# Softmax maxima for one quad of channels in eight, kept on the chip instead of sent through memory for two; reordered start and end of a two-layer product-quantised convolution

## The chip, the cores and the metric

One core of one Trainium2 chip. The metric is device time in microseconds (us) of one execution; medians are over several executions on the chip. The kernel before takes 2812.78 us, the median of four runs (2811.74 in three of them). Verdicts are drawn at 2%, which is 56 us here.

The engines are called by their names: TensorE (PE in the profile), VectorE (DVE), ScalarE (ACT), GpSimd (POOL) and SyncE (SP). PSUM is the accumulator memory that TensorE writes, SBUF the on-chip memory that holds this kernel's other tiles. The granted clock is the share of TensorE's full clock that the profile records; at half clock it is 0.5.

## The reference

16 images of 256 channels and 28 x 28 positions. A convolution layer is replaced by a soft choice among 16 centroids per channel; two layers follow each other.

```python
def amm_conv3x3(x, centroids, w_sub):          # (B,256,28,28), (256,16,9), (256,9,256)
    p = patches3x3(x)                            # B, n=784, c=256, s=9
    d = sum(p*p) - 2 * einsum('bncs,cks->bnck', p, centroids) + sum(centroids**2)
    attn = softmax(-d, axis=-1)                  # over the 16 centroids
    lut  = einsum('cks,cso->cko', centroids, w_sub)
    return einsum('bnck,cko->bno', attn, lut)
xn = group_norm(x)                               # 32 groups of channels
out = relu(bn1(amm_conv3x3(xn, centroids1, wsub1)))
out = bn2(amm_conv3x3(out, centroids2, wsub2))
out = se_gate(out)                               # mean -> 16 -> 256 -> sigmoid, a scale per channel
return x + relu(out + xn)
```

The `sum(p*p)` term is the same for all centroids and drops out of the softmax. What has to be computed per position and channel is 16 logits, their exponentials, 9 weighted sums (called numerators) and one total.

## The kernel before

Each image and layer is cut into two position tiles (384 and 400 columns) and each of these into eight quads of channels. One quad of one tile is a *unit*, and the kernel advances one unit per *slot* of about 4.9 us. For a unit, TensorE computes the logits as a group of 32 small matmuls (32 x 32 tiles of the array) into two pairs of PSUM banks, ScalarE exponentiates, TensorE computes the numerators as another group of 32, VectorE transposes them out of PSUM, inverts the totals, GpSimd multiplies (`k`), VectorE transposes back (`q`), and TensorE multiplies `q` with the output weights into the accumulator ("looks", groups of 128 x 128 matmuls). Several units are in flight at once.

There are only three PSUM pairs, and logits and numerators take two each in turn:

```python
ring = [p_ring.tile([P, 2, 512], F32, name=f"pair{i}") for i in range(3)]
def pair():
    turn[0] += 1
    return ring[turn[0] % 3]
```

So the second half of a unit's logits always needs the pair that the first of the two numerator transposes (`nt<-pair` in the profile) of the unit ahead has emptied.

In the second layer the logits can be large, and for two quads of eight the exponentials need their maxima subtracted. The kernel before computes the logits of these units twice: once early to find the maxima, which go through memory and come back as two more rows of the patches (21 and not 19), and once more for use. Units whose maxima are subtracted are called *treated* below.

```python
if m in maxed:                                   # MAXED = (0, 4)
    a = s - self.lb                              # lb = 6 slots ahead
    at(a, MAX, a_logits, u);  at(a, MAX, a_turn, u)            # logits, transposed
    at(a + 1, TURN_BACK, a_max, u, 0)
    at(a + 2, TURN_BACK, a_max, u, 1);  at(a + 2, TURN_BACK, m_turn, u)
    at(a + 3, MOVE, m_out, u);  at(a + 4, MOVE, m_in, u)       # through memory
at(s, LOGITS, b_logits, u);  at(s, EXP, b_exp, u)              # again, with maxima
at(s + 1, NUM, b_num, u)
at(s + 1, TURN, b_turn, u);  at(s + 1, TURN, c_scale, u)       # nt, rc, k
at(s + 2, TURN_BACK, c_turn, u)                                # q
```

Within a slot the positions run in the order LOGITS, EXP, LOOK_A, NUM, TURN, LOOK_B, MAX, LOOK_C, TURN_BACK, REST.

## Time and profile before

| | before |
|---|---|
| median (with the changed kernel's runs) | 2812.78 us (2810.43 to 2818.25) |
| span of the profiled run, granted clock | 2814.8 us, 0.990 |
| busy: TensorE, VectorE, GpSimd, ScalarE | 98%, 80%, 63%, 39% |
| second-layer logits computed twice | 16 images x 2 tiles x 2 quads = 64 units |

```profile
PE acc L717 <- ACT im L729: 2.3, 1, 2.3
PE pair L585 <- DVE nt L665: 1.9, 3, 1.0
```

The first line holds the 64 extra groups (2048 of the 18432 matmuls). The wait of logits for the numerator transposes is 1.9 us in the whole run.

### The profile page before, as it was taken

What the parts mean: (1) busy time and instruction counts of PE and PEld (TensorE: products, weight loads), DVE (VectorE), ACT (ScalarE), POOL (GpSimd) and SP (SyncE); (2) the same over time, 40 slices, a digit from 0 to 9 for tenths busy, and PEclk for the clock granted to TensorE, in tenths of its full rate; (3) what the DMA queues carried; (4) which work ended last, traced back from release to release, by engine and by line L of the source; (5) the groups of instructions that cost most, each with busy time, mean ns of one, the idle gap of its engine ahead of it and who ended that gap; (6) DMA issues with size and microseconds to landing.
All of it is one profiled execution on the core that took longest, in us unless ns stands there. A gap on an engine that the chain in (4) does not pass through costs nothing.

```text
span 2814.8 us, 94692 instructions
## 1 busy us (share of the span) xinstructions
PE 2756.0 (98%) x39794; PEld 1090.2 (39%) x39794; DVE 2252.0 (80%) x2772; ACT 1086.5 (39%) x1595; POOL 1782.1 (63%) x2589
## 2 busy tenths in 40 slices
PE   6999999999999999999999999999999999999996
PEld 3333333333333343333333333343333334333332
DVE  4668788887878878788887878878788887878885
ACT  2333433434334343433434334343433434334332
POOL 3785666756666575665756667575665756665653
PEclk9999999999999999999999999999999999999998
DMA  8787878768687676777777687676777767674641
GB/s 223 205 202 193 234 204 225 194 169 219 155 226 195 167 212 165 214 184 191 191 175 218 159 222 195 169 214 161 215 189 191 190 170 221 161 210 106 163 122 55
DMA packets 292787, 525.83 MB, mean 187 GB/s; under 512 B 94096, under 2 KB 247552, under 8 KB 292352
## 3 DMA queue, kind: packets, MB, share of 16 engines
q0 software_dynamic: 51808, 269.48, 36.0%
q1 hardware_dynamic: 240544, 250.20, 34.5%
q8 instruction: 315, 5.16, 0.8%
q14 instruction: 120, 0.98, 0.1%
HBM read 267.87 MB, written 251.69 MB: 185 GB/s over the span
## 4 chain that ended last, share of the span: by engine, by line
PE 92%; DVE 3%; POOL 2%; DMA 2%; issue 1%; ACT 0%; SPq 0%; DVEq 0%; POOLq 0%; ACTq 0%
PE acc L717 58%; PE pair L585 17%; PE pair L653 15%; DVE nt L665 1%; POOL k L681 1%; DMA pt<-pat 1%; DVE q L699 0%; DMA pat<-side 0%; DVE rc L671 0%; PE pair L319 0%; DMA out_dram<-y 0%; POOL pat L486 0%; PE pair L514 0%; POOL total L693 0%; DVE gn_st L434 0%
## 5 line engine op out<-in xcount | busy, mean ns | idle before, releaser
L717 PE MATMUL acc<-q,ws 128*128 128x384 f32 (+1 forms) x4096 | 1645.9, 520 | 5.1 <-ACT y L739 2.8
L681 POOL TENSOR_TENSOR k<-nt,rc 128x832 f32<-128x832 f32 (+1 forms) x512 | 802.9, 1568 | 980.6 <-DVE rc L671 970.7
L665 DVE STREAM_TRANSPOSE nt<-pair 128x832 f32<-128x832 f32 (+1 forms) x1024 | 979.3, 994 | 487.3 <-PE pair L653 436.0
L643 ACT ACTIVATE e<-pair 128x800 f32<-128x800 f32 (+1 forms) x1024 | 787.5, 821 | 1356.8 <-PE pair L585 1303.2
L717 PEld LDWEIGHTS acc<-q,ws 128*128 128x128 f32 x4096 | 698.1, 190 | 903.2 <-issue 577.6
L585 PE MATMUL pair<-pt,wd 19*32 19x384 f32 (+2 forms) x18432 | 556.6, 501 | 11.4 <-DMA pt<-pat 8.2
L699 DVE STREAM_TRANSPOSE q<-k 128x832 f32<-128x832 f32 (+1 forms) x512 | 488.9, 955 | 0.8 <-POOL k L681 0.8
L653 PE MATMUL pair<-e,cw 32*32 32x384 f32 (+1 forms) x16384 | 485.5, 501 | 0.3 <-DVE nt L665 0.2
L671 DVE RECIPROCAL rc<-nt 128x104 f32<-128x104 f32 (+1 forms) x512 | 398.5, 778 | 17.6
L585 PEld LDWEIGHTS pair<-pt,wd 19*32 19x32 f32 (+1 forms) x18432 | 138.2, 103 | 339.8 <-issue 276.2
L687 POOL TENSOR_TENSOR tail<-nt,rc 128x104 f32<-128x104 f32 (+1 forms) x512 | 236.7, 462 | 0.0
L653 PEld LDWEIGHTS pair<-e,cw 32*32 32x32 f32 x16384 | 119.9, 103 | 289.5 <-issue 154.8
L717 PE MATMUL acc<-qt,ws 128*128 128x400 f32 (+1 forms) x512 | 219.3, 510 | 0.0
L693 POOL TENSOR_TENSOR total<-total,nt 128x96 f32<-128x96 f32 (+1 forms) x448 | 197.4, 441 | 0.0
L486 POOL DMA_DIRECT2D pat<-side x274 | 184.7, 674 | 3.5 <-ACT side L475 3.0
L693 POOL TENSOR_TENSOR total<-total,rc 128x96 f32<-128x96 f32 (+1 forms) x448 | 176.1, 393 | 0.0
L717 PEld LDWEIGHTS acc<-qt,ws 128*128 128x128 f32 x512 | 91.1, 190 | 100.1 <-issue 50.3
L609 DVE TENSOR_REDUCE mx<-z 128x48 f32<-128x768 f32 (+1 forms) x128 | 120.6, 942 | 0.0
L604 DVE STREAM_TRANSPOSE z<-pair 128x768 f32<-128x768 f32 (+1 forms) x128 | 118.1, 961 | 0.0
L486 POOL DMA_DIRECT2D pat<-im x136 | 92.0, 677 | 0.7 <-ACT side L475 0.6
L739 ACT ACTIVATE y<-acc,bnsh,bnsc 128x384 f32<-128x384 f32 (+1 forms) x64 | 43.3, 677 | 87.3 <-PE acc L717 81.6
L551 POOL TENSOR_TENSOR y<-y,xt 128x392 f32<-128x392 f32 x60 | 65.9, 1099 | 10.4 <-ACT y L547 10.4
(113 smaller groups left out, 720.5 us busy)
## 6 DMA issues: line engine op xcount, KB each, us to landing
pat<-side POOLq DMA_DIRECT2D x232, 588.0 KB, 6.0
pt<-pat SPq DMA_DIRECT2D x1024, 112.5 KB
pt<-pat SPq DMA_DIRECT2D x1024, 108.0 KB
pat<-im POOLq DMA_DIRECT2D x116, 588.0 KB, 5.9
xt<-in_x POOLq DMA_DIRECT2D x32, 784.0 KB, 8.1
out_dram<-y POOLq DMA_DIRECT2D x16, 784.0 KB, 6.1
pat<-side POOLq DMA_DIRECT2D x24, 300.0 KB, 5.3
pat<-side POOLq DMA_DIRECT2D x18, 288.0 KB, 5.5
```

The costliest lines, as they stand in the source:

```text
L486: eng.dma_start(view(pat, (ROWS * p0 + 9 * k + 3 * dx) * HW + px, [[ROWS * HW, m], [HW, 3], [1, n]]), bass.AP(v.tensor, v.offset, [list(v. ...
L585: nc.tensor.matmul(ps[t // 2][c : c + 32, t % 2, :n], lhsT=wd[l][32 * i : 32 * i + rows, 4 * u["m"] + t, :], rhs=u["pt"][32 * i : 32 * i + ...
L609: nc.vector.tensor_reduce(u["mx"][:, 2 * v : 2 * v + 2].rearrange("p t (j b) -> p t b j", j=2)[:, :, :nb], u["z"].pop(0)[:, : 64 * nb].rea ...
L643: nc.scalar.activation(e[:, :, :n], ps[:, :, :n], AF.Exp, scale=2.0)
L653: nc.tensor.matmul(u["nm"][t // 2][32 * i : 32 * i + 32, t % 2, :n], lhsT=cw[l][c : c + 32, 4 * u["m"] + t, :], rhs=es[t // 2][c : c + 32, ...
L665: nc.vector.transpose(nt[:, :nb, 2 * v : 2 * v + 2].rearrange("p b t r -> p t b r"), ps[:, :, : 32 * nb].rearrange("p t (b r) -> p t b r", ...
L671: nc.vector.reciprocal(rc[:, : 8 * nb], u["nt"][:, :, SUM])
L681: nc.gpsimd.tensor_tensor(q[:, :nb].rearrange("p b (a s) -> p (b a) s", s=8), nt[:, :, :8], rc.unsqueeze(2).to_broadcast([P, 8 * nb, 8]), ...
L687: nc.gpsimd.tensor_tensor(tails[key][:, :nb, 8 * (m % 4) : 8 * (m % 4) + 8], nt[:, :, 8].rearrange("p (b a) -> p b a", a=8), rc.rearrange( ...
L693: nc.gpsimd.tensor_add(t[:, : 8 * nb], t[:, : 8 * nb], v)
L699: nc.vector.transpose(q[:, :, : 32 * nb].rearrange("p h (b r) -> p h b r", r=32), u.pop("k")[:, :nb].rearrange("p b (h r) -> p h b r", h=2),)
L717: nc.tensor.matmul(accs[key][:, :n], lhsT=ws[l][:, 2 * m + h if h < 2 else 2 * NQ + m // 4, o * P : (o + 1) * P], rhs=u["q"][h][:, :n], st ...
```

## The change

The intent: treat one quad of eight and not two; compute its logits once, and subtract the maxima from the transposed copy on the chip; and trim the start (first image's normalisation ahead of the sorting of channels, first patches alone on the queues) and the end (last image gated and stored by block, the check of the sums moved ahead). A bar on the centroids lessens the logits so that the other quads stay in range without maxima.

```diff
-MAXED = (0, 4)
+MAXED = (0,)
...
                     if m in maxed:
                         a = s - self.lb
-                        at(a, MAX, a_logits, u)
+                        at(a, MAX, logits, u)
                         at(a, MAX, a_turn, u)
-                        at(a + 1, TURN_BACK, a_max, u, 0)
-                        at(a + 2, TURN_BACK, a_max, u, 1)
-                        at(a + 2, TURN_BACK, m_turn, u)
-                        at(a + 3, MOVE, m_out, u)
-                        at(a + 4, MOVE, m_in, u)
+                        for v in range(2):
+                            at(a + 1 + v, TURN_BACK, a_max, u, v)
+                            at(a + 2 + v, REST, a_less, u, v)      # GpSimd: z - max
+                        at(s - 1, TURN_BACK, a_back, u, 0)         # VectorE: transpose back
+                        at(s, EXP, a_back, u, 1)
+                        at(s, EXP, a_exp, u)                       # from SBUF
                     else:
                         self.loads.append((s - self.lead, s, u))
-                    at(s, LOGITS, b_logits, u)
-                    at(s, EXP, b_exp, u)
+                        at(s, LOGITS, logits, u)
+                        at(s, EXP, b_exp, u)
...
-    load_x(0, x[0])                                   # GpSimd's queue
+    load_x(0, x[0], nc.sync)
...                                                    # statistics ahead of the sorting
-    plan = Plan(1, 3, 6)
+    plan = Plan(1, 3, 5)
...
-            plan.prep(0, pat_of(0, b), {1: 9, ...}, 0.67 if b == 1 else 1)
+            if b == 1: plan.prep_near(0, pat_of(0, b), 9)      # second image's patches by tile
...
-    plan.at(14, REST, square_codes, 1)                # second codes' setup between slots
-    plan.at(15, REST, setup_codes, 1)
...                                                    # last image: close_last, store_block
```

Cut: the new sort key and bar, the placement of the second codes, the spreading of early patch writes, the guard's second program.

## The prediction

> **What bounds the kernel now.** I read the page first (busy shares), then TensorE's timeline in the middle of the run, then its waits, then VectorE's timeline beside it, and last the head and the tail.
>
> ```profile
> PE 2756.0 (98%) x39794; PEld 1090.2 (39%) x39794; DVE 2252.0 (80%) x2772; ACT 1086.5 (39%) x1595; POOL 1782.1 (63%) x2589
> ...
> PE 92%; DVE 3%; POOL 2%; DMA 2%; issue 1%; ACT 0%; SPq 0%; DVEq 0%; POOLq 0%; ACTq 0%
> ```
>
> TensorE carries 92% of the chain that ended last. A high busy share alone could hide gaps, so the timeline has to show whether groups follow each other without a hole. This is TensorE (start, duration) around one extra logits group of the second layer:
>
> ```profile
> 1599.01 1.61 PE L717 MATMUL acc<-q,ws 128*128 128x400 f32 x4
> 1600.55 0.95 PE L585 MATMUL pair<-pt,wd 19*32 19x400 f32 x32
> 1601.43 1.61 PE L717 MATMUL acc<-q,ws 128*128 128x400 f32 x4
> 1602.97 0.93 PE L585 MATMUL pair<-pt,wd 19*32 19x384 f32 x32
> ```
>
> No idle bracket. A logits group (32 instructions, 16 at a time) takes 0.88 us from start to next start at 400 columns, 0.86 at 384. An accumulation group of four takes 1.54 us; elsewhere six take 2.21, so two more cost 0.67 and each group pays about 0.21 us of entry beside its matmuls. The image period comes from the chain of work, where the same piece recurs every 169.21 us:
>
> ```profile
> 978.09 2.21 PE acc L717 x6
> ...
> 1147.30 2.21 PE acc L717 x6
> ...
> 1665.90 2.21 PE acc L717 x6
> 1835.11 2.21 PE acc L717 x6
> ```
>
> 16 x 169.21 = 2707 of the 2815 us. The other 107 us are head, tail and a few stalls. Per image: 68 groups of 32 at about 0.87 = 59; 144 looks at 0.655 = 94; 68 entries at 0.21 = 14; small norm and gate matmuls 1.4; sum 168.7. So the steady part has no stall to remove: a saving must be TensorE work.
>
> VectorE is second, with 80%. Its unit of work per slot (one tile of one quad, about 4.9 us of TensorE) is two transposes out of PSUM, a reciprocal, one transpose back:
>
> ```profile
> 1599.20 1.85 DVE L665 STREAM_TRANSPOSE nt<-pair 128x768 f32<-128x768 f32 x2 [0.77 <-PE pair L653]
> 1601.08 0.76 DVE L671 RECIPROCAL rc<-nt 128x96 f32<-128x96 f32 x1
> 1601.75 1.91 DVE L604 STREAM_TRANSPOSE z<-pair 128x832 f32<-128x832 f32 x2
> 1603.59 0.94 DVE L699 STREAM_TRANSPOSE q<-k 128x768 f32<-128x768 f32 x1
> ```
>
> It waits 0.77 us for TensorE before the pair: one and a bit us of slack in a quiet slot, no more. And where VectorE is late, TensorE does stop. This is the last image, where four gate operations came first:
>
> ```profile
> 2733.93 2.67 DVE L543 SCALAR_TENSOR_TENSOR y<-xt,gn_rstd,y 128x392 f32<-128x392 f32 x4
> 2736.53 1.83 DVE L665 STREAM_TRANSPOSE nt<-pair 128x768 f32<-128x768 f32 x2
> ...
> 2742.55 1.97 DVE L665 STREAM_TRANSPOSE nt<-pair 128x832 f32<-128x832 f32 x2
> ```
>
> ```profile
> 2742.25 0.90 PE L585 MATMUL pair<-pt,wd 19*32 19x400 f32 x16
> 2743.64 0.91 PE L585 MATMUL pair<-pt,wd 19*32 19x400 f32 x16 [0.49 <-DVE nt L665]
> 2744.48 1.56 PE L717 MATMUL acc<-q,ws 128*128 128x384 f32 x4
> ```
>
> The second half of the logits needs the PSUM pair that the first of the two transposes empties. The transposes began 0.30 us after the logits, so logits to next group took 2744.48 - 2742.25 = 2.23 us in place of 0.88: 1.35 us lost. This price list returns below.
>
> **What the Trainium skill says.** "TensorEngine Tiling (Array Packing)", Key Properties: changing the tiling mode drains the engine. The 0.21 us per group agrees, since every group here alternates between 32x32 and 128x128. The same page, PSUM Bottleneck: tiling speeds up TensorE but not the emptying of PSUM; the 2742 us lines show it. "TensorE: Matmul & The Clock Gate", What's actually happening: after an idle window of some 3.4 us the array runs at half clock until it has been busy about as long. The stretch 36 to 46 us has a granted clock of 0.5 to 0.6 after a 6 us wait for patches. "DMA: Bandwidth & Descriptors", Queues, rings and completion order: an engine takes packets from its queues in turn, so what shares the time with the first patches delays them; the trace (12.26 us from the last issue to landing) fits.
>
> **The change part by part.**
>
> *Second-layer maxima, TensorE.* Before, quads 0 and 4 each compute logits twice per tile: 16 images x 2 tiles x 2 quads = 64 extra groups. After, quad 0 alone is treated, and its only logits group is turned, lessened by its maxima, turned back and exponentiated from SBUF; quad 4 is plain. All 64 extra groups go, and with each one entry, since two look groups merge. 64 x (0.87 + 0.21) = 69 us off the path.
>
> *The same, VectorE.* Gone: 64 units x (1.85 transposes + 1.89 maxima + 0.31 small turn) = 259 us. Added or kept: 32 units x (1.85 + 1.85 + two transposes back, about 1.8) = 176. Net 83 us less, on average a relief. But it is not spread. The order of VectorE's instructions in the built new kernel puts both transposes back directly after one slot's regular work and directly ahead of the next slot's pair, while the next slot is also shorter, because it has no logits group. I work one such place out by hand. Let N be the start of the numerator group ahead of it, 400 columns. VectorE: pair at N+1.08 (as 1598.15 to 1599.20 above), reciprocal +2.01, transpose +0.72, then free +0.92: N+4.73. Two transposes back, 0.84 each at the spacing of the existing SBUF ones: N+6.41, and only then the next pair. TensorE: 0.88 + four merged looks 2.88 + numerator 0.88 + two looks 1.54: next logits at N+6.19. The transposes thus begin 0.2 to 0.3 us after the logits, the very case of 2742 us: first transpose 1.09, second half group 0.83, so the next group starts at N+8.33 in place of N+7.05. Loss 1.28 us; at 384 columns the same sum gives 1.27. 32 x 1.27 = 41 us back.
>
> *GpSimd.* Added: 64 subtractions of 128x832 at about 1.57 (as the k product, same shape) = 100 us, and 32 x 0.84 of totals for quad 4; 1782 becomes about 1900, 69% of the span. In the slots that also hold the residual and the store it lags about 1.2 us, and the second subtraction still ends about 1.2 us before it is needed. Off the path.
>
> *Transfers.* The 64 round trips of the maxima through memory go. They were hidden.
>
> *Head.* x leads SyncE's queue and the statistics come first on VectorE: apply at about 15.4 us in place of 18.25. Patches then share the engines with the other six patch writes instead of the next x: land at about 30 to 31 in place of 35.4. They still trickle into TensorE, some 4 us. Gain 4. Slots 0 to 5 keep their GpSimd wait for the centroid scratch (6.07 us) and the half clock: 1. The setup of the second codes (6 matmuls 1.88 us, wait 1.09) leaves TensorE at 137 to 140 us, but the patch loads that queue behind the centroid placements are already late there (wait 1.71 us, then half clock), and two placements are added: of 3.5 I credit 2.
>
> *Tail.* From the last gate at 2796.5 VectorE now has six operations at about 0.62 instead of eight (5.0 us): 1.3; the check of the sums moves ahead; the store goes by block from SyncE instead of after GpSimd's residual (2802.78) with 0.73 of issue: together about 4. Other waits around the first image: 1.5.
>
> Sum: -69 + 41 - 4 - 1 - 2 - 4 - 1.5 = -40.5 us from 2811.7, so about 2770, or 1.5% less.
>
> **The rivals.**
>
> First, no new stall: VectorE's load falls, and the author spread the work over five slots. Then -69 and the ends give about 2730 (2.9% less). For it: 80% busy, waits of 0.8 to 2.4 us in quiet slots. Against it: the order of instructions and the 1.35 us already seen. Half the stall gives 2750.
>
> Second, GpSimd becomes late: a subtraction that runs 1.5 us longer than the k product, or lags more, holds the transposes back and, in order behind them, all of VectorE. Each further us costs 32 us: about 2800. Against it: the same shape was timed at 1.57 us.
>
> Third, the ends give more: without the half-clock ramps 15 to 20 us could go. Against it: TensorE still waits about 5 us for its patches. That gives about 2758.
>
> Fourth, the guard: if the sums of the now unmaxed quad left their bounds, everything would be computed again and the time would about double. I computed the sums for the given inputs; they lie from 7e-21 to 1.3e26, inside 1e-26 to 1e32. Not expected.
>
> **Range and chances.** The work removed is nearly certain (69, give or take 3). The stall is 41 with 25 below and 20 above; the ends 12, give or take 8. So 2770, from 2740 to 2790. Two per cent less is 2755.5: it needs the stall at about two thirds or less, or rich ends, chance 0.26. Slower by 2% needs the second rival in a strong form, 0.02.
>
> **What would show each step.** TensorE logits instructions 18432 to 16384. A period of about 169.2 - 4.3 + 2.5 = 167.4 us per image; without the stall 164.9. In TensorE's waits, logits waiting for the numerator transposes some 30 times, half to one us each, twice per image and just after the slot without logits, with the two transposes back ahead on VectorE. First logits near 34 us. From the last accumulation to the end about 17 to 18 us where it was 21. I am wrong if that wait is absent (the time is then near 2730), or if VectorE waits there for GpSimd's subtraction.

## More of the kernel before

The experiments ran in three batches on three chips, each beside the kernel before, whose medians there were 2814.72, 2816.78 and 2812.83 us; so a difference between medians of different batches can be off by some us.

The groups of instructions that the change touches, on the page of the kernel before (line, engine, operation, output and input, count, then busy us and mean ns of one, then idle time ahead of them and who ended most of it), followed by two lines of TensorE's list of waits (us in total, times, longest):

```profile
L585 PE MATMUL pair<-pt,wd 19*32 19x384 f32 (+2 forms) x18432 | 556.6, 501 | 11.4 <-DMA pt<-pat 8.2
L604 DVE STREAM_TRANSPOSE z<-pair 128x768 f32<-128x768 f32 (+1 forms) x128 | 118.1, 961 | 0.0
```

## The result, and the profile after

| | before | after |
|---|---|---|
| median | 2812.78 us (2810.43 to 2818.25, 4 runs) | 2775.06 us (2772.23 to 2776.79, 4 runs) |
| ratio, 95% interval | | 0.9862, 0.9845 to 0.9879 |
| profiled run, clock | 2814.8 us, 0.990 | 2770.4 us, 0.992 |
| logits matmuls | 18432 | 16384 |
| busy: TensorE, VectorE, GpSimd | 98%, 80%, 63% | 97%, 79%, 69% |

A ratio is the mean time of one kernel's runs over that of the other's of the same rounds, so it is not quite the ratio of the medians quoted. The time falls by 37.7 us in the medians and by 44.4 between the two profiled runs (the profiled run of the kernel before took 2816.25 us, 3.5 above its median, that of the changed kernel 2772.23, 2.8 below); so small effects below are read inside the traces. A repeat of the unaltered changed kernel in a later batch, whose expectation was

> The changed kernel once more, unaltered, so that the three runs beside it are compared on the same chip: both theories expect 2770 to 2778, ratio near 0.986, 32 waits of logits for the numerator transposes.

gave 2773.62 us and the ratio 0.9859 (0.9839 to 0.9879).

The page of the changed kernel, its logits group, and the first lines of TensorE's waits that have to do with the change:

```profile
PE 2700.0 (97%) x37748; PEld 1080.9 (39%) x37748; DVE 2178.4 (79%) x2641; ACT 1091.2 (39%) x1591; POOL 1912.0 (69%) x2730
...
L598 PE MATMUL pair<-pt,wd 19*32 19x384 f32 (+1 forms) x16384 | 513.5, 501 | 23.5 <-DVE nt L672 16.1
```

```profile
PE pair L598 <- DVE nt L672: 16.1, 32, 3.0
...
PE pair L598 <- DMA pt<-pat: 7.5, 1, 7.5
PE acc L724 <- ACT im L736: 6.2, 1, 6.2
```

The first wait is the predicted one: exactly 32 times, which is 16 images x 2 tiles. The longest, 3.0 us, is in the last image, where four other operations of VectorE stand ahead of the pair too; the other 31 are 0.41 to 0.43 us each. The total of 16.1 us must not be taken for what it costs. Here is one place on TensorE, then the same stretch on VectorE (start, duration, line, count, and in brackets the idle time that the profile records):

```profile
1605.84 1.56 PE L724 MATMUL acc<-q,ws 128*128 128x384 f32 x4
1607.32 0.90 PE L598 MATMUL pair<-pt,wd 19*32 19x400 f32 x16
1608.63 0.91 PE L598 MATMUL pair<-pt,wd 19*32 19x400 f32 x16 [0.41 <-DVE nt L672]
1609.47 2.20 PE L724 MATMUL acc<-q,ws 128*128 128x384 f32 x6
```

```profile
1602.40 1.85 DVE L672 STREAM_TRANSPOSE nt<-pair 128x768 f32<-128x768 f32 x2 [1.82 <-PE pair L660]
...
1604.95 0.92 DVE L706 STREAM_TRANSPOSE q<-k 128x768 f32<-128x768 f32 x1
1605.79 1.92 DVE L636 STREAM_TRANSPOSE e<-z 128x832 f32<-128x832 f32 x2
1607.64 1.80 DVE L672 STREAM_TRANSPOSE nt<-pair 128x768 f32<-128x768 f32 x2
```

Logits start to next group start is 1609.47 - 1607.32 = 2.15 us, where an undisturbed group takes 0.88: 1.27 us lost, of which the profile calls only 0.41 idle. All 31 equal places show it: 2.11 to 2.15 us, so 1.25 to 1.27 lost. (A split group shows as two rows of 16, each about as long as a whole row of 32, because both halves of an undisturbed group run beside each other.) On VectorE no bracket appears after the 1.82 us at 1602.40: from there it works without a gap, and the two transposes back (`e<-z`, 1.85 us from start to next start) stand right ahead of the transposes that would have freed the pair.

The image period, from the chain of work of the changed kernel:

```profile
1306.18 2.21 PE acc L724 x6
...
1473.53 2.21 PE acc L724 x6
...
1640.87 2.21 PE acc L724 x6
```

167.35 us, where it was 169.21. The removed work without the stall would give 167.35 - 2 x 1.27 = 164.8.

Where the 44 us of the trace arose, by marks on TensorE that both kernels have:

| mark | before, at us | after, at us | ahead by | 
|---|---|---|---|
| first logits | 38.47 | 38.44 | 0.0 |
| seventh unit's logits | 79.30 | 77.66 | 1.6 |
| first logits of the second image | 140.54 | 129.40 | 11.1 |
| an accumulation early in image 1 of layer 2 | 311.96 | 301.95 | 10.0 |
| statistics of the last image | 2340.22 | 2307.54 | 32.7 |
| last accumulation starts | 2792.66 | 2750.22 | 42.4 |
| end of the span | 2814.8 | 2770.4 | 44.4 |

Four things there were not predicted: no gain at the first logits, over 9 us between the seventh unit and the second image, and a loss of 1.1 us ahead of the fourth mark, although images were already getting shorter, and, from the last image's statistics to the last accumulation, 9.7 us where 2.7 periods would give 5.0. For the first, the chain of waits of the changed kernel has this line:

```profile
27.16 11.14 DMA pt<-pat
```

The patches are written 8 us earlier than before (27.2 against 35.5 us), but then the twelve loads of them take 11.1 us, where before they took 2.8. For the third, ScalarE at 200 us:

```profile
200.19 0.67 ACT L736 ACTIVATE im<-acc,bnsh,bnsc 128x384 f32<-128x384 f32 x1 [11.54 <-DMA pat<-im]
```

An accumulator can't be evacuated because patch writes still read the buffer that it goes to. TensorE stands for 6.2 us and then runs its next group at half clock (2.96 us to the next start for four matmuls that take 1.54). For the fourth, the kernel before has a stop in the last image that the changed kernel doesn't have; no run takes this part of the gain apart:

```profile
2757.48 3.04 PE L717 MATMUL acc<-q,ws 128*128 128x400 f32 x4 [2.81 <-ACT y L739]
```

### The profile page after: what moved, and what is told of

It reads as the page before. It is cut to its first block, busy times and chain, and to the rows that moved or that the text cites.

```text
span 2770.4 us, 90183 instructions
## 1 busy us (share of the span) xinstructions
PE 2700.0 (97%) x37748; PEld 1080.9 (39%) x37748; DVE 2178.4 (79%) x2641; ACT 1091.2 (39%) x1591; POOL 1912.0 (69%) x2730
## 4 chain that ended last, share of the span: by engine, by line
PE 86%; DVE 8%; issue 3%; POOL 1%; DMA 1%; ACT 0%; DVEq 0%; SPq 0%; ACTq 0%; POOLq 0%
PE acc L724 55%; PE pair L598 16%; PE pair L660 15%; DVE nt L672 3%; DVE q L706 1%; DVE rc L678 1%; DVE e L636 1%; DMA pt<-pat 0%; POOL k L688 0%; PE pair L331 0%; DMA pat<-side 0%; POOL pat L494 0%; PE pair L522 0%; DVE gn_st L442 0%; DMA pat<-im 0%
## 5 line engine op out<-in xcount | busy, mean ns | idle before, releaser
L650 ACT ACTIVATE e<-pair 128x768 f32<-128x768 f32 (+1 forms) x960 | 740.5, 821 | 1039.9 <-PE pair L598 1037.1
L598 PE MATMUL pair<-pt,wd 19*32 19x384 f32 (+1 forms) x16384 | 513.5, 501 | 23.5 <-DVE nt L672 16.1
L598 PEld LDWEIGHTS pair<-pt,wd 19*32 19x32 f32 x16384 | 124.7, 103 | 332.5 <-issue 240.6
L700 POOL TENSOR_TENSOR total<-total,nt 128x96 f32<-128x96 f32 (+1 forms) x480 | 213.3, 444 | 0.0
L494 POOL DMA_DIRECT2D pat<-side x286 | 193.1, 676 | 2.6 <-issue 1.4
L700 POOL TENSOR_TENSOR total<-total,rc 128x96 f32<-128x96 f32 (+1 forms) x480 | 188.3, 392 | 0.0
L643 ACT ACTIVATE e<-e 128x768 f32<-128x768 f32 (+1 forms) x64 | 54.9, 857 | 190.1 <-DVE e L636 188.7
L736 ACT ACTIVATE im<-acc,bnsh,bnsc 128x384 f32<-128x384 f32 (+1 forms) x64 | 43.4, 678 | 149.8 <-PE acc L724 137.9
L628 POOL TENSOR_TENSOR z<-z,mx 128x768 f32<-128x768 f32 (+1 forms) x64 | 99.0, 1547 | 0.0
```

Of the source, the lines that this page charges most:

```text
L494: eng.dma_start(view(pat, (ROWS * p0 + 9 * k + 3 * dx) * HW + px, [[ROWS * HW, m], [HW, 3], [1, n]]), bass.AP(v.tensor, v.offset, [list(v. ...
L598: nc.tensor.matmul(ps[t // 2][c : c + 32, t % 2, :n], lhsT=wd[l][32 * i : 32 * i + rows, 4 * u["m"] + t, :], rhs=u["pt"][32 * i : 32 * i + ...
L628: nc.gpsimd.tensor_tensor(z, z, mx.unsqueeze(2).to_broadcast(list(z.shape)), ALU.subtract)
L650: nc.scalar.activation(e[:, :, :n], ps[:, :, :n], AF.Exp, scale=2.0)
L700: nc.gpsimd.tensor_add(t[:, : 8 * nb], t[:, : 8 * nb], v)
```

## The experiments

Theory: the stall of about 1.27 us at 32 places gives back some 40 of 69 us, and it comes from where VectorE's instructions stand. Rivals: VectorE and GpSimd have too much to do in these slots wherever it stands; or the listed waits (16 us) are all there is. Further theories concern the head, the stretch at 195 us and the end. All experiments are edits of the changed kernel, and all gave correct results; ratios are to the kernel before.

| run | median us | ratio (95%) | profiled span | period |
|---|---|---|---|---|
| changed kernel | 2775.06 | 0.9862 (0.9845 to 0.9879) | 2770.4 | 167.35 |
| second transpose back after the pair | 2778.74 | 0.9872 (0.9853 to 0.9890) | 2777.1 | 167.8 |
| a whole transpose back more | 2830.52 | 1.0055 (1.0036 to 1.0073) | 2828.3 | |
| half a transpose back more | 2799.64 | 0.9951 (0.9931 to 0.9971) | 2799.6 | 168.59 |
| transposes back a slot earlier | 2741.54 | 0.9738 (0.9723 to 0.9753) | 2738.9 | 165.41 |
| whole chain a slot earlier | 2739.35 | 0.9740 (0.9722 to 0.9759) | 2736.9 | 164.94 |
| second x on SyncE's queue | 2769.56 | 0.9835 (0.9820 to 0.9851) | 2768.8 | |
| middle tap's patches earlier | 2772.19 | 0.9854 (0.9834 to 0.9874) | 2767.8 | |
| second image's patches as before | 2782.70 | 0.9881 (0.9866 to 0.9896) | 2781.0 | |
| flag early | 2767.91 | 0.9829 (0.9815 to 0.9842) | 2766.0 | |
| combination 1 | 2731.69 | 0.9702 (0.9688 to 0.9717) | 2727.4 | |
| combination 2 | 2738.59 | 0.9739 (0.9719 to 0.9760) | 2736.9 | |

### Second transpose back behind the next pair (a miss)

```diff
-                        at(s, EXP, a_back, u, 1)
-                        at(s, EXP, a_exp, u)
+                        at(s, EXP, a_exp, u, 0)          # exponential of the first half
+                        # in b_turn of the same slot: nt, nt, a_back(u, 1), a_exp(u, 1), reciprocal
```

> The changed kernel with only the order of one VectorE operation changed: of the two transposes back of a treated unit, the second is put behind the next numerator pair's two transposes out of PSUM, ahead of that pair's reciprocal, so that one and not two stands directly ahead of the pair; the exponential is split by half accordingly. No work is added or taken. My theory (the stall comes from the order, two operations of 0.9 us standing ahead of the pair that frees PSUM): the 32 waits of logits for the numerator transposes go or fall to a handful, the period falls from 167.35 to about 165 us per image, the time from 2775 by some 35 to 41 us to 2734 to 2740. Rival (VectorE with GpSimd simply has too much to do in these slots, so that any order is late): the wait moves to the next group (accumulation waiting for q, or numerators waiting for e), the period stays at 167.3 or nearly, the time stays within 8 us of 2775. Between, near 2755: the second transpose back now delays the chain of reciprocal and q and costs about half.

Nothing was gained: 2778.74 us, and the period rose to 167.8. The waits of TensorE and one place (same columns as above):

```profile
PE pair L666 <- ACT e L656: 10.6, 33, 0.8
```

```profile
1612.24 1.29 PE L598 MATMUL pair<-pt,wd 19*32 19x400 f32 x32
1613.46 2.20 PE L735 MATMUL acc<-q,ws 128*128 128x384 f32 x6
1615.59 0.90 PE L666 MATMUL pair<-e,cw 32*32 32x400 f32 x16
1616.85 0.91 PE L666 MATMUL pair<-e,cw 32*32 32x400 f32 x16 [0.35 <-ACT e L656]
1617.68 1.56 PE L735 MATMUL acc<-q,ws 128*128 128x384 f32 x4
```

The logits now take 1.22 us in place of 2.15, but the numerators of the treated unit itself, one group later, take 2.09 in place of 0.88, because their exponentials come late. The rival had named just this: the wait moves. My theory in the form "two operations ahead are too many, one is not" fell. What remained open was whether VectorE has no time at all there, or only none in these two slots.

### More of the suspected work: a whole and a half transpose back

```diff
                         at(s, EXP, a_back, u, 1)
+                        at(s, EXP, a_back_again, u, 1)   # the same tile, the same values
```

> The changed kernel with the second transpose back done twice (the same tile written again with the same values): three and not two transposes of about 0.9 us stand ahead of the pair, at all 32 places. My theory (every microsecond of VectorE ahead of the pair at these places is a microsecond of TensorE, because there is no slack left at them): 32 x 0.84 to 0.92 = 27 to 29 us more, about 2803, the wait of the logits 32 times and about 1.3 us each in place of 0.5. Rival (the waits that the trace lists are only 16 us in sum and the rest of the gap to the 69 us is something else, such as mode switches or a slower clock): the time grows by 10 us or less.

It cost twice what I expected: 2830.52 us, 55 more than the changed kernel. The waits and one place:

```profile
PE pair L598 <- DVE nt L675: 49.5, 32, 4.1
```

```profile
1639.43 0.91 PE L598 MATMUL pair<-pt,wd 19*32 19x400 f32 x16 [1.49 <-DVE nt L675]
1640.26 3.89 PE L727 MATMUL acc<-q,ws 128*128 128x384 f32 x6
```

The waits grew by 49.5 - 16.1 = 33.4 us, 1.04 per place for an operation of 0.97 us. But the six matmuls after the wait took 3.83 us (to 1644.09), where they take 2.13 at full clock. The granted clock in stretches of 4 us (a row gives the length, the busy time and count of each engine from TensorE to GpSimd, then the granted clock, the busy share of the transfer engines and GB/s):

```profile
1634.00:1638.00 4.00, 3.94 (x55) 1.23 (x53) 3.97 (x5) 0.87 (x1) 3.98 (x7) 1.00 0.90 194
1638.00:1642.00 4.00, 2.57 (x19) 1.31 (x20) 3.83 (x5) 3.05 (x4) 1.41 (x2) 0.79 0.93 285
1642.00:1646.00 4.00, 4.00 (x39) 1.63 (x39) 0.84 (x1) 0.00 (x0) 2.38 (x5) 0.79 0.81 215
```

0.79 in each of two stretches is (1 - 0.79) x 8 / 0.5 = 3.4 us at half clock. So a wait of 1.5 us was followed by a spell of half clock. I compared the group behind each wait with its usual length: 13 of the 31 waits of 1.44 to 1.49 us (the 32nd, in the last image, is longer) were followed by a slow spell of about 1.65 us more, some 21 us together; with the 33.4 that makes 54 of the 55. The mean clock fell from 0.992 to 0.985. The trace's record of the granted clock shows more: all its half-clock spells start at whole multiples of 3.41 us from one another, and the 13 stops are exactly those that began 0.64 to 1.69 us after such a beat; the other 18 began 1.73 to 2.94 us after one. So in this trace the place in the beat decided which stops cost a spell.

Half the dose was to separate the two:

```diff
+    def a_back_again(u, v):                              # half the tile
+        nc.vector.transpose(u["e"][v][:, 0, : 32 * blocks(u)], u["z"][v][:, : 32 * blocks(u)])
```

> The changed kernel with half a transpose back (128x384 or 128x416, about 0.5 us) repeated ahead of the pair at all 32 places. The whole one cost 55 us: 33 us of longer waits and some 20 us of half clock after 12 of the 32 waits of 1.5 us. Theory (each microsecond of VectorE there is a microsecond of TensorE, and the clock falls only when the stop is long): waits of about 0.9 us, 32 x 0.46 = 15 us more, 2787 to 2793, mean granted clock 0.99 as without. Rival (the clock loses in proportion to the stop, so half the dose costs half of 55): 2800 to 2805, clock 0.988.

2799.64 us, 26 more than the repeat of the changed kernel on the same chip (2773.62), so the number came out next to the rival's range (2800 to 2805), near half of 55. The composition is another:

```profile
PE pair L598 <- DVE nt L675: 36.2, 32, 3.7
```

The waits grew by 36.2 - 16.1 = 20.1 us (to 1.05 us each), and only 3 of those 31 were followed by a slow spell, about 1.65 us each and 4.9 together. (Here the beat alone does not part them: spells followed stops that began 0.95, 1.06 and 1.32 us after one, none those at 1.08 and 1.27.) The period without a slow spell is 168.59, 0.62 more per place for an operation of 0.50 us. So neither expectation was right: the clock loses far less than in proportion, while the wait grows by about 0.1 us more than the operation in both doses. Where this 0.1 us comes from the runs don't show. What both doses do show is that these places have no slack: VectorE's time there is TensorE's time.

### The transposes back in the slots before

```diff
-                        at(s - 1, TURN_BACK, a_back, u, 0)
-                        at(s, EXP, a_back, u, 1)
+                        for v in range(2):
+                            at(s - 2 + v, TURN_BACK, a_back, u, v)
-    tpool (treated logits) bufs=3, epool (exponentials) bufs=4
+    tpool bufs=2, epool bufs=5
```

> The changed kernel with the two transposes back of a treated unit one slot and half a slot earlier: the first before the pair of the slot ahead (where VectorE waits 1.8 us for TensorE in the trace of the changed kernel), the second alone ahead of the pair at the place of the stall; for this the exponentials' tiles become five and the treated logits' two (space). Same operations, same number. The first order experiment only moved the wait from the logits to the numerators. Theory now (VectorE has too much in these two slots and idle time in the one before: placement across slots, not throughput): the waits of logits for the numerator transposes and of numerators for e are gone or below 0.2 us, the period falls from 167.35 to about 164.9, the time from 2775 by 35 to 41 us to 2734 to 2740. Rival (VectorE and GpSimd are saturated over the whole stretch of five slots, or five exponential tiles block ScalarE): a wait of the same size comes back elsewhere and the time stays within 10 us of 2775.

2741.54 us, 33.5 less than the changed kernel and 2.6% less than the kernel before. The same two slots, TensorE and then VectorE:

```profile
1589.34 1.56 PE L724 MATMUL acc<-q,ws 128*128 128x384 f32 x4
1590.83 1.22 PE L598 MATMUL pair<-pt,wd 19*32 19x400 f32 x32
1591.97 2.20 PE L724 MATMUL acc<-q,ws 128*128 128x384 f32 x6
```

```profile
1584.00 1.00 DVE L636 STREAM_TRANSPOSE e<-z 128x832 f32<-128x832 f32 x1
1585.83 1.85 DVE L672 STREAM_TRANSPOSE nt<-pair 128x768 f32<-128x768 f32 x2 [0.83 <-PE pair L660]
...
1589.23 1.00 DVE L636 STREAM_TRANSPOSE e<-z 128x832 f32<-128x832 f32 x1
1590.15 1.80 DVE L672 STREAM_TRANSPOSE nt<-pair 128x768 f32<-128x768 f32 x2
```

Of the waits of logits for the numerator transposes one is left, in the last image:

```profile
PE pair L598 <- DVE nt L672: 2.0, 1, 2.0
```

The first transpose back has moved into a gap in which VectorE waited 1.8 us for TensorE (0.83 of it is left), and the logits take 1.14 us instead of 2.15. With the same operations in the same number, 31 of 32 waits are gone from the list. (The two pools changed size with it; that alone was not run.) That decides between placement and throughput: VectorE was not short of time, it was short of time in two slots. The period fell to 165.41, by 1.94 of the 2.54 us that were lost. (Ten of twelve image periods are 165.41. One is 165.71; the 165.71 and 0.62 us in the next expectation come from that one image.) The rest is 0.32 us at the other tile's place and 0.27 at this one, with no idle recorded at either.

### The whole chain a slot earlier

```diff
-                            at(s - 2 + v, TURN_BACK, a_back, u, v)
+                            at(s - 2, TURN_BACK, a_back, u, v)
-    plan = Plan(1, 3, 5)
+    plan = Plan(1, 3, 6)                                  # and the first patches one slot earlier
```

> The changed kernel with the treated unit's whole chain one slot earlier (logits six slots ahead, not five) and both transposes back in the slot two ahead, where VectorE waits 1.8 us for TensorE and two of 0.92 just fit; nothing extra is left ahead of the last two pairs. Exponentials' tiles five, treated logits' tiles two, as in the earlier experiment, whose image period was 165.71 with 0.62, 0.27 and 0.39 us still lost per image at three groups. Theory (placement alone): these three vanish too, period 164.4, 16 x 2.94 = 47 us less than the changed kernel, of which the last image keeps 3: 2728 to 2733. Rival (some of it is throughput of VectorE or GpSimd): the period stays at 165.5 or more and the time at 2740 or more.

The period became 164.94, so both remaining losses went (one other logits group of each image now takes 1.03 us in place of 0.88). (The third that I had listed, 0.39 us, stayed, and I had misread it: it is a wait of 0.32 us for the normalisation's statistics, and the kernel before has it too.) The prediction had put the period without the stall at 164.9. The time, 2739.35, did not follow: the earlier chain needs the first second-layer patches a slot earlier, and in the crowded stretch at 160 us this made a new wait. ScalarE there:

```profile
160.11 0.82 ACT L483 COPY side<-im 128x756 f32<-128x756 f32 x1 [8.07 <-DMA pat<-side]
```

Behind this copy stand the exponentials for which TensorE then waits 5.8 us.

### The head: the second image's x

```diff
-            plan.at(n0 - 8, REST, load_x, b, x[b])                 # for b == 1
+            plan.at(n0 - 8, REST, load_x, b, x[b], nc.sync)        # behind the first patch loads
```

> The changed kernel with only the load of the second image's x moved from GpSimd's queue (issued at 22 us, while the first patches' loads wait) to SyncE's queue behind these loads. Theory (the four microseconds of the head were lost because the twelve first patch loads shared the transfer engines with this load, 11.1 us from the writes' landing to theirs in place of 2.8): the patches land 3 to 4 us earlier, first logits at 34 to 35 us in place of 38.4, the time 3 to 4 us less than 2775. Rival (they are slowed by the other six patch writes, or by their own many small packets): first logits stay at 37.5 to 38.5 and the time within 1 us.

First logits at 33.98 us in place of 38.44, and their last part done 4.2 us earlier: the load of 784 KB beside the first patches was what ate the head's gain. At the first stalled place, though, TensorE is only 1.4 us ahead (225.92 against 227.28): the set-up group behind the first logits took 8.05 us in place of 6.56, since more of it fell into half clock (granted clock 0.50 from 38 to 42 us and 0.83 from 42 to 46), and the rest went later. The medians say 5.5 us less, the traces 1.6; the runs don't settle which is nearer.

### The stretch at 195 us

```diff
-                    s = t1 if dx == 1 else ...
+                    s = t1 - 3 if dx == 1 else ...                 # middle tap's patches, first and last image
```

> The changed kernel with only the second layer's first patch writes of the middle tap column (the tile of 400) issued three slots earlier for the first and the last image, so that the evacuation of an accumulator at about 195 us, which overwrites their source, doesn't wait for them. Theory (this wait of 6.2 us, with the half clock after it, is a cost that the change brought, 2.3 us before): the wait at 195 us goes, image 1 starts 6 to 9 us earlier, the time 6 to 9 us less, about 2767. Rival (what is late there is the whole queue, so that another wait takes its place, for pat or for the patch loads): TensorE stops 3 us or more in the same stretch and the time falls by 2 us or less.

The wait of the evacuation is gone, and a smaller one for the patch loads took its place. TensorE:

```profile
191.22 2.45 PE L598 MATMUL pair<-pt,wd 19*32 19x384 f32 x32 [0.17 <-ACT im L736]
...
196.23 2.82 PE L598 MATMUL pair<-pt,wd 19*32 19x400 f32 x32 [1.07 <-DMA pt<-pat]
```

At the first stalled place TensorE is 4.0 us ahead (223.26 against 227.28), at the end 2.6; in the last image, where the same edit acts, patch loads come late (0.65 us of wait at 2626). So the truth lies between the two expectations: the wait was a real cost of the change, about half of it returns in another form.

### The second image's patches as before

```diff
-                plan.prep_near(0, pat_of(0, b), 9)
+                plan.prep(0, pat_of(0, b), 9, 0.67)               # whole at once
```

> The changed kernel with the second image's patches written as before the change (whole at once, paced at two thirds of a slot) and not by tile. Theory (the 9.5 us that the changed kernel gained between slots 6 and 16 over my estimate of 2 come in part from these writes no longer delaying the patch loads on SyncE's queue): late patch loads and a half clock come back at 100 to 135 us and 5 to 8 us are lost, about 2781. Rival (they come from the setup of the second codes that left TensorE and VectorE at 137 to 140 us, and from later gathers): the time stays within 2 us of 2775 and the wait for patches near 125 us stays away.

2782.70 us, 7.6 more in the medians and 10.6 between the profiled runs. TensorE at 135 us, where the changed kernel has no wait:

```profile
135.01 1.86 PE L598 MATMUL pair<-pt,wd 19*32 19x384 f32 x4 [3.53 <-DMA pt<-pat]
137.62 2.78 PE L598 MATMUL pair<-pt,wd 19*32 19x384 f32 x28 [0.75 <-DMA pt<-pat]
```

The first logits of the second image end at 140.33 - the start of the next group - where the changed kernel is there at 130.26: about as late as the kernel before. So the unexpected 9.5 us between the seventh unit and the second image hang on this one line, the writing of the second image's patches by tile; it also changes the pace of the writes, and the run doesn't part the two.

### The flag at the end

```diff
+    plan.at(t + NS + LC - 1, REST, judge)   # matmul, count, bad: as soon as the sums are complete
...
-    ... count, bad after the last gate
```

> The changed kernel with the flag of the guard (a matmul, a sum, one comparison) computed as soon as its sums are complete, ahead of the last image's gating, and not after it. Theory (the end follows the flag: some 11.3 us from the flag's last operation to the end in both kernels, so the store was never what set the end): the end moves up by 4 to 9 us relative to the last accumulation, until the store's landing (about 2761 in the changed kernel's trace) sets it; 2766 to 2771. Rival (the end follows the last work of any engine, or the store's landing with a fixed closing time): the time stays within 1.5 us of 2775.

2767.91 us. From the last accumulation to the end of the span 16.0 us are left (2750.04 to 2766.0) where it was 20.2. In the changed kernel the flag's last operation is at 2758.93 and the end 11.5 us after it, in the kernel before at 2803.41 with 11.4 after it (first two lines); here it stands ahead of the gates (last two), and the end is 7.9 us after the start of VectorE's last operation:

```profile
2803.41 0.14 DVE L935 TENSOR_SCALAR bad<-count 1x1 int32<-1x1 f32 x1
```

```profile
2758.93 0.14 DVE L974 TENSOR_SCALAR bad<-count 1x1 int32<-1x1 f32 x1
```

```profile
2751.21 0.14 DVE L903 TENSOR_SCALAR bad<-count 1x1 int32<-1x1 f32 x1
...
2758.09 0.57 DVE L563 SCALAR_TENSOR_TENSOR y<-y,xt 128x392 f32<-128x392 f32 x1
```

So it was the branch on the flag that set the end of the changed kernel, and not the store. For the kernel before, the same 11.4 us speak for it, but no run tested it.

### Combinations

The first joins the earlier transposes back, the second x on SyncE's queue, the middle tap's patches and the early flag:

> The changed kernel with the earlier transposes back, the second image's x on SyncE's queue (5 us measured alone), the middle tap column's patches three slots earlier (3 us measured alone) and the early flag together. If the parts add: 41 + 5 + 3 + 5 = 54 us less than 2775, about 2721, 3.3% less than the kernel before. If the stall only moves again: 2760 to 2768.

2731.69 us, 2.98% less than before: faster than both kernels. It is 10 us short of the sum that I wrote down, and that is because the 41 us were not all there: by the traces the earlier transposes back give 31.5 us at the last accumulation, the two transfers 7.0 more, the flag 4.5; 43.0 together, and the span fell from 2770.4 to 2727.4.

The second takes the whole chain a slot earlier in place of the first's placement:

> The earlier chain of the treated units with the other three (second image's x on SyncE's queue, middle tap column's patches three slots earlier, early flag). The combination before took 2731.7, of which the traces gave 31.5 to the transposes back, 7 to the two transfers and 4.4 to 5 to the flag. Theory: another 16 x 1.28 = 20 us, less 2 to 3 for the last image: 2713 to 2716, ratio 0.964. Rival: 2728 or more.

2738.59 us, a miss: the shorter period is there, but the middle tap's earlier patches and the earlier chain crowd the last image's transfers. TensorE waits at two places, and the granted clock from 2580 to 2620 us is 0.87:

```profile
2587.86 0.92 PE L598 MATMUL pair<-pt,wd 19*32 19x384 f32 x26 [2.15 <-DMA pt<-pat]
...
2594.15 1.63 PE L598 MATMUL pair<-pt,wd 19*32 19x400 f32 x26 [1.19 <-DMA pt<-pat]
```

The wait of 4.8 us for exponentials near 158 us is there as well. The first combination is the best version that was run.

## Why the prediction was right

The time (2775.06 in place of 2770, inside the range) and the two large terms were right in mechanism and size.

- **The removed logits, -69 us.** 2048 fewer matmuls, as said. Without the stall the period would be 164.8 (164.94 reached with the chain a slot earlier), so 4.3 to 4.4 us per image or 68 to 71 in all.
- **The stall, +41 us.** 31 places of 1.25 to 1.27 us, 39 in all, and the one in the last image, which is longer. The net period of 167.4 was predicted and 167.35 found. Half to one us of recorded wait was foretold for each; it is 0.41. That the cause is where VectorE's instructions stand is shown by moving them (33.5 us back) and by adding to them (each us there costs at least a us).
- **What the first reason left out.** In planning the first experiment I took it that two operations ahead of the pair are too many. The order experiment shows that to take one of them behind the pair helps nothing, since the treated unit's own numerators then wait. The condition is wider: both have to be done before the slot begins.
- **The head, 4 us: wrong.** The step that failed is "patches then share the engines with the other six patch writes instead of the next x". They shared them with the next x too, which GpSimd issued at 22 us. Its removal brought the first logits to 34.0, the number predicted.
- **Slots 0 to 5, 1 us:** 1.6.
- **Up to the second codes, 2 us: mis-sized.** 9.5 us, because I charged the late patch loads to the centroid placements, which the change keeps. They came from the second image's patch writes, which it spreads.
- **Around the first image, 1.5 us: wrong in sign.** The wait of 2.3 us at the evacuation became 6.2 us with half clock after it. I had not looked at what the moved patch writes read.
- **The tail, 4 us:** 2.0 in the traces. The step that failed is the store "by block from SyncE" as part of the gain: the branch on the flag set the end, so in the changed kernel an earlier store alone could not move the end.
- **The last image: not foreseen.** About 4.8 us, behind the stop of 2.8 us that is gone; its cause stays open.
- **A sum.** The rounded terms of the image period add to 168.4 and not 168.7, unrounded to 169.2, the measured one; nothing rests on it.

The errors at the ends (4 + 1.5 + 2 us promised and not given, and the 1.1 us lost at 195 us, against 7.5 more than credited and 4.8 not foreseen) largely cancel, which is luck. Of the rivals, "no new stall" is refuted by the 32 waits; "GpSimd late" did not occur, its subtraction took 1.55 us where 1.57 was assumed, and the transposes back never wait for it in the lines shown; the guard was not entered.

## What to carry to other kernels

When work is taken off the busiest engine and a part of it handed to the second busiest, look up in the built order where each new instruction stands relative to the one that frees the first engine's next buffer; the mean busy share (79%) said nothing about two slots that had no gap. Price a stop from group start to group start and not from the recorded idle time (1.27 us against 0.41), and look for the gap in an earlier slot before reordering within the full one. At start and end, ask what else is on the transfer engines at that moment, and what the last instruction really waits for.

## What the Trainium skill lacked or had wrong

- "TensorE: Matmul & The Clock Gate", What's actually happening, gives an idle window of about 3.4 us before the clock halves. Here stops of 1.44 to 1.49 us were followed by half clock in 13 of 31 cases, stops of 1.05 us in 3 of 31, and stops of 0.41 to 0.43 us in none of 31. The spells lasted 3.41 us and started on a beat of 3.41 us, which agrees with the page's window, free-running as it says. But a stop well under the window can cost a spell, and with the longer stops the place in the beat decided it (0.64 to 1.69 us after it: yes; 1.73 to 2.94: no). The page's section on PSUM-queue cycling does speak of short idles that make the clock swing, but gives them no length.
- "TensorEngine Tiling (Array Packing)", Key Properties, says that a change of tiling mode drains the engine but gives no figure. A group costs about 0.21 us of entry beside its matmuls (worked out in the prediction); how much of it is the drain no run shows.
- "Perfetto Trace Analysis", Optimization Strategy, says that consistent bubbles can mean too few SBUF or PSUM buffers. The 31 equal gaps fit, since the logits lacked a PSUM pair; but the cure here needed no PSUM, only an earlier place for two VectorE instructions (33.5 us). The page doesn't name this case.
- The pages have figures for a single branch instruction and for a register load, but none says how long a program takes to end once it branches on a value computed at its end. From the flag's last operation to the end were 11.4 and 11.5 us in the two kernels, and to compute the flag 8 us earlier shortened the end by 4.2 us.
